# Two 48-row A loads of block 0, moved from one DMA issuing queue to two

## The chip, the cores and the metric

The kernel runs on one core of one Trainium2 chip. The metric is device time in microseconds (us) of one execution; lower is better. Before the change three runs gave a median of 473.93 us, between 473.69 and 474.05.

## The reference, cut to what matters

The input `x` is 8 batches of 256 tokens with 1024 features. Every batch b picks a low-rank adapter (rank 16) by `itok_B_3_7[b]`; the adapted activations go through a gated feed-forward network whose inputs are rounded to 8 bits; the result is added to `x`.

```python
def cond(x, A, B, ids):                    # A: 8 x 1024 x 16, B: 8 x 16 x 1024
    Bx = jnp.einsum('bni,bri->bnr', x, B[ids])
    return jnp.einsum('bnr,bor->bno', Bx, A[ids])

def linear(x, w_q, in_scale, w_scale):     # fp8 rounding of the input
    x_q = jnp.clip(x / in_scale, -448, 448).astype(jnp.float8_e4m3fn)
    return jnp.einsum('bsh,ih->bsi', x_q.astype(jnp.float32) * in_scale, w_q * w_scale)

h = cond(x, A, B, ids)
hidden = jax.nn.silu(linear(h, gate_w, ...)) * linear(h, up_w, ...)   # 2752 wide
return x + linear(hidden, down_w, ...)
```

## The kernel before

The 2048 tokens are four blocks of 512 (t = 0 to 3), two batches to a block. Features stand on the 128 partitions, so a block of `x` is eight slices (k = 0 to 7) of 128 x 512 floats. Everything is computed in transposed form. For one block the work is:

1. `bx`: B times x, summed over k = 0 to 7 (rank 16, so small matmuls). For block 0 this is `two_times_b`. It needs all of x of block 0 and the two B tiles of its two batches.
2. `bm`: VectorE and ScalarE copy `bx` out of PSUM, in two steps, to lie under the A rows (lines 570 and 574).
3. `c`: A times bm, in `two_times_a`: 32 matmuls, 64 in the trace since each float32 product is two passes. Weights are rows of `a_two[0]`. Those rows hold A of the two batches: batch 0 in rows 0 to 47, batch 1 in rows 80 to 127. Each is one load of 48 rows of 2 KB, 96 KB. The row groups are taken in the order 0, 2, 1, 3, so the first matmul needs the load of batch 0, the next one that of batch 1.
4. `xg`: ScalarE and VectorE round `c` to fp8 (lines 608 and 606).
5. `gate_up(c, t)`: for each of 22 column chunks c of the 2752, 16 matmuls of 128x128 by 512 against streamed weights `w_gu` (1 MB a chunk), then silu and a product into `hid`.
6. A last part multiplies `hid` by the down weights and adds `x`.

TensorE is busy from the start. Before the data of block 0 are there it runs fillers on ones (`pass_time` into `warm`): 14 at the start, two between k = 6 and k = 7, and six after `bx`, ahead of `c`. Matmuls keep the program's order on TensorE. On the other engines a planner at compile time chooses the order, by the program's order and by when it thinks that an instruction's inputs are there.

At the start the loads are issued by two queues. ScalarE's queue issues the adapter numbers `ids_i`, a small read `touched` of the first weights, and B of batch 0 (behind a register load of its adapter number). SyncE's queue issues all else, in the order: x slices 0-1, x slices 2-4, B of batch 1 (behind its register load), x slices 5-6, x slice 7, A of batch 1, then a second register load and A of batch 0, then the weight loads, of which the first four are halves of chunks 0 and 1. The two A loads are `load_a_two` (L398 to L402) and its two calls at L443 and L444. x slices 0-1, 2-4, 5-6 and 7 are separate loads of 512, 768, 512 and 256 KB. Ahead of the A loads GpSimd sets `a_two[0]` to zero (L384).

Each load announces its landing on a completion counter. Loads issued by ScalarE and SyncE take the counters in turn, and an issue waits, on its own queue, until the earlier load on the same counter has landed.

Of the kernel before, what the change touches and what calls it, by code (L numbers as in the profile page):

```python
# [301 lines left out]
def adaln_ffn(  # L302
# [15 lines left out]
    nc = tc.nc  # L318
# [45 lines left out]
    with ExitStack() as fast:  # L364
# [5 lines left out]
        xs = [acts.tile([P, NH, TB], F32, name=f"x{t}") for t in range(NTB)]  # L370
# [8 lines left out]
        b_two = [lora.tile([P, 2 * BROW + R], F32, name=f"b{t}") for t in range(2)]  # L379
        a_two = [lora.tile([P, H // 2], F32, name=f"a{t}") for t in range(2)]  # L380
# [7 lines left out]
        def adapter_of(batch, queue):  # L388
            return queue.value_load(ids_i[0:1, batch : batch + 1], min_val=0, max_val=7)  # L389

        def load_b(b, i, adapter, queue):
            load = queue.dma_start(  # L392
                out=b[:, i * BROW : (i + 1) * BROW], in_=b8[bass.ds(adapter * P, P), :]
            )
            if queue is nc.gpsimd:
                tc.keep_in_program_order(load)

        def load_a_two(j, adapter):  # L398
            row = 2 * 32 * j + R * j
            nc.sync.dma_start(  # L400
                out=a_two[0][row : row + 3 * R], in_=a8[bass.ds(adapter * 3 * R, 3 * R), :]
            )  # L402

# [7 lines left out]
        def load_x(t, k):  # L411
            piece, first = x_of(x4, t, k)
            ks = slice(first, first + piece.shape[1])
            nc.sync.dma_start(out=xs[t][:, ks, :], in_=piece)  # L414
# [16 lines left out]

        load_x(0, 0)
        load_x(0, 2)
        load_b(b_two[0], 0, adapter_of(0, nc.scalar), nc.scalar)
        touched = const.tile([R, R], F32, name="touched")
        nc.scalar.dma_start(
            out=touched, in_=gate_up_of(w_gu, 0).rearrange("(r g) n -> r g n", r=R)[:, 0, :R]
# [1 line left out]
        second = adapter_of(1, nc.sync)  # L439
        load_b(b_two[0], 1, second, nc.sync)  # L440
        load_x(0, 5)
        load_x(0, 7)
        load_a_two(1, second)  # L443
        load_a_two(0, adapter_of(0, nc.sync))  # L444
        for c in range(NFIRST):
            load_gate_up(c, parts=(0, 2, 4) if c < 2 else (0, 4))
        adapters = [adapter_of(2 + q, nc.gpsimd if q < 2 else nc.sync) for q in range(6)]
# [442 lines left out]
        for k in range(NH - 1):  # L890
# [23 lines left out]
            first = k % 2 == 0  # L914
# [133 lines left out]
```

## Time and profile before

| what | value |
|---|---|
| median of three runs | 473.93 us |
| the profiled execution | 473.77 us |
| its span on the core | 472.1 us |
| TensorE (PE) busy | 467.3 us, 99% of the span, 2477 matmuls |
| ScalarE (ACT) busy | 194.9 us, 41% |
| VectorE (DVE) busy | 106.5 us, 23% |
| GpSimd (POOL) busy | 16.0 us, 3% |
| bytes moved by DMA | 56.01 MB, mean 119 GB/s |
| DMA in the first 40 us | mean 371 GB/s |

The profiled execution is 1.67 us longer than its span: this much lies around what the profile covers. Times inside the profile count from the start of the span. In a line of the timeline the first number is the start, the second the duration, "x2" the instructions merged into the line, and the bracket the idle time of the engine before it and what ended that.

The loads of the start, from the timeline (issue) and the view of DMA issues (time from issue to landing):

| load | queue | issue at | issue to landing |
|---|---|---|---|
| adapter numbers | ScalarE | 0.86 | not listed; the register loads that wait for it start at 2.06 |
| x slices 0-1, 512 KB | SyncE | 0.86 | 3.4 |
| x slices 2-4, 768 KB | SyncE | 1.29 | 4.9 |
| `touched`, 1 KB | ScalarE | 1.46 | 3.8 |
| B of batch 0, 68 KB | ScalarE | 3.01 | 3.5 |
| B of batch 1, 68 KB | SyncE | 3.06 | 3.7 |
| x slices 5-6, 512 KB | SyncE | 3.46 | 4.4 |
| x slice 7, 256 KB | SyncE | 3.94 | 5.0 |
| A of batch 1, 96 KB | SyncE | 4.65 | not listed |
| A of batch 0, 96 KB | SyncE | 5.80 | 4.0 |
| chunk 0, first half, 512 KB | SyncE | 6.23 | 4.9 |

### The profile page before, as it was taken

To read this page: it belongs to the slowest core of one execution; us is meant where nothing else is said; L and a number is where in the kernel's file an instruction comes from. 1 tells how busy PE (TensorE), PEld (TensorE's weight loads), DVE (VectorE), ACT (ScalarE), POOL (GpSimd) and SP (SyncE) were. 2 spreads that over 40 slices of the span, in tenths; PEclk is the share of its full clock that TensorE was granted. 3 is DMA by queue.
4 is the path that set the end of the run, shared out by engine and by line. 5 is a ranking of instruction groups with operands and counts; after the bars stand their busy time and mean duration, and the time that the engine had idled before them with its cause. 6 is when DMAs were issued, how large, how long until landed. Compare 5 with 4: busy or idle time off the path is not lost.

```text
span 472.1 us, 5981 instructions
## 1 busy us (share of the span) xinstructions
PE 467.3 (99%) x2477; PEld 214.5 (45%) x2477; DVE 106.5 (23%) x170; ACT 194.9 (41%) x257; POOL 16.0 (3%) x32
## 2 busy tenths in 40 slices
PE   8999999999999999999999999999999999999997
PEld 4454444444444444444444444444444444444444
DVE  1314341222121212212122121231120111031031
ACT  2315258996655554553345545359112012021000
POOL 0230500000000000000000000000000000000000
PEclk9999999999999999999999999999999999999999
DMA  8999205352222211222220021132435345163031
GB/s 303 422 369 367 53 3 169 104 173 89 90 89 90 89 30 61 89 90 89 90 87 20 27 62 57 61 105 102 136 115 161 77 174 162 40 207 104 5 115 68
DMA packets 14661, 56.01 MB, mean 119 GB/s; under 512 B 1762, under 2 KB 2786, under 8 KB 11938
## 3 DMA queue, kind: packets, MB, share of 16 engines
q1 hardware_dynamic: 14256, 55.08, 34.2%
q8 instruction: 21, 0.34, 0.3%
q0 software_dynamic: 192, 0.40, 0.3%
q14 instruction: 14, 0.11, 0.1%
q10 hardware_dynamic: 178, 0.07, 0.1%
HBM read 47.15 MB, written 8.39 MB: 118 GB/s over the span
## 4 chain that ended last, share of the span: by engine, by line
PE 97%; DMA 1%; SPq 0%; issue 0%; DVE 0%
PE y L521 63%; PE yd L521 32%; PE c L521 1%; PE bx L521 1%; DMA x<-x 1%; DMA ids_i<-ids 0%; SPq L389 0%; PE warm L521 0%; SPq L392 0%; SPq L414 0%; DVE o L855 0%; PE count L521 0%
## 5 line engine op out<-in xcount | busy, mean ns | idle before, releaser
L521 PE MATMUL y<-xg,w_gu 128*128 128x512 fp8e4 x1376 | 298.6, 379 | 0.0
L521 PEld LDWEIGHTS <-w_gu 128*128 128x128 bf16 x1376 | 133.7, 98 | 162.0 <-DVE xg L606 1.6
L521 PE MATMUL yd<-hid,w_d 128*128 128x512 fp8e4 (+2 forms) x693 | 146.0, 373 | 0.0
L695 ACT ACTIVATE g<-y,gate_s 128x512 f32<-128x512 f32 (+1 forms) x88 | 59.5, 681 | 134.1 <-PE y L521 134.1
L724 DVE SCALAR_TENSOR_TENSOR hid<-y,up_by_down,g 128x512 fp8e4<-128x512 f32 x84 | 63.0, 750 | 215.9 <-PE y L521 145.7
L521 PEld LDWEIGHTS <-w_d 128*128 128x128 bf16 x693 | 66.6, 98 | 79.0 <-issue 1.7
L507 ACT ACTIVATE junk<-w_d 128x1408 bf16<-128x1408 uint16 (+1 forms) x16 | 21.2, 1323 | 88.3 <-DMA w_d<-w_d 88.2
L855 DVE SCALAR_TENSOR_TENSOR o<-yd,down_s,x 128x512 f32<-128x512 f32 x28 | 20.0, 748 | 107.5 <-PE yd L521 93.4
L507 ACT ACTIVATE junk<-w_gu 128x2048 bf16<-128x2048 uint16 (+1 forms) x22 | 41.0, 1864 | 0.0
L514 ACT ACTIVATE junk<-hid 128x2048 bf16<-128x2048 fp8e4 x21 | 40.1, 1908 | 0.6
L514 ACT ACTIVATE junk<-xg 128x2048 bf16<-128x2048 fp8e4 x8 | 15.3, 1911 | 0.3
L606 DVE TENSOR_SCALAR xg<-c,inv 128x512 fp8e4<-128x512 f32 (+1 forms) x20 | 11.7, 638 | 6.4 <-PE c L521 6.4
L608 ACT ACTIVATE xg<-c,inv 128x512 fp8e4<-128x512 f32 (+1 forms) x20 | 10.6, 601 | 4.6 <-PE c L521 4.6
L521 PE MATMUL warm<-const-bfloat16-1.0 128*128 128x512 bf16 (+1 forms) x22 | 5.9, 426 | 0.9 <-PEq L1037 0.9
L855 DVE SCALAR_TENSOR_TENSOR o<-yd,down_s,xg 128x512 f32<-128x512 f32 (+2 forms) x5 | 3.2, 644 | 12.3 <-PE yd L521 9.9
L507 ACT ACTIVATION_READ_ACCUMULATOR junk<-w_gu 128x1 f32 x22 | 4.2, 193 | 0.0
L521 PEld LDWEIGHTS <-const-bfloat16-1.0 128*128 128x128 bf16 x23 | 2.3, 118 | 4.3 <-issue 3.8
L521 PE MATMUL yd<-hid_tail,w_dt 64*128 64x512 bf16 (+1 forms) x32 | 4.2, 377 | 0.0
L724 DVE SCALAR_TENSOR_TENSOR tail<-y,up_by_down,g 64x512 fp8e4<-64x512 f32 x4 | 3.0, 756 | 4.9 <-ACT g L695 4.8
L514 ACT ACTIVATION_READ_ACCUMULATOR junk<-hid 128x1 f32 x21 | 3.9, 187 | 0.0
L521 PE MATMUL bx<-x,b_four_twice 128*32 128x256 f32 x64 | 3.7, 380 | 0.0
L521 PE MATMUL bx<-x,b 128*32 128x128 f32 x64 | 2.3, 277 | 0.9 <-DMA b<-b 0.7
(69 smaller groups left out, 56.1 us busy)
## 6 DMA issues: line engine op xcount, KB each, us to landing
w_gu<-w_gu SPq DMA_DIRECT2D x18, 1024.0 KB, 4.9
outT<-o SPq DMA_DIRECT2D x31, 256.0 KB, 2.1
w_d<-w_d SPq DMA_DIRECT2D x8, 704.0 KB, 5.1
w_gu<-w_gu SPq DMA_DIRECT2D x10, 512.0 KB, 4.9
w_d<-w_d SPq DMA_DIRECT2D x8, 640.0 KB, 3.8
x<-x SPq DMA_DIRECT2D x2, 2048.0 KB, 19.3
x<-x SPq DMA_DIRECT2D x1, 1792.0 KB, 13.8
x<-x SPq DMA_DIRECT2D x2, 512.0 KB, 3.9
```

The costliest lines, as they stand in the source:

```text
L507: nc.scalar.activation(junk_like(w), low(w), AF.Copy, accum_out=lows[:rows, column : column + 1])
L514: nc.scalar.activation(junk_like(q), q, AF.Square, accum_out=squares[:rows, column : column + 1])
L521: tc.keep_in_program_order(nc.tensor.matmul(*args, **kwargs))
L606: nc.vector.tensor_scalar(to, c, scale, None, ALU.mult, saturate=False)
L608: nc.scalar.activation(to, c, AF.Copy, scale=scale, saturate=False)
L695: nc.scalar.activation(g[rows], gates, AF.Silu, scale=gate_s[: gates.shape[0]])
L724: nc.vector.scalar_tensor_tensor(to, in0=ups, scalar=up_by_down[rows], in1=g[rows], op0=ALU.mult, op1=ALU.mult, saturate=False,)
L855: nc.vector.scalar_tensor_tensor(o, in0=y, scalar=down_s, in1=x, op0=ALU.mult, op1=ALU.add)
```

## The change

`load_a_two` takes the issuing queue as an argument. A of batch 1 stays on SyncE's queue behind all of x. A of batch 0 goes to ScalarE's queue, and uses the register that ScalarE loaded for B of batch 0, so SyncE's second register load disappears. Ahead of it ScalarE copies one element of x slice 2 into the first element of `a_two[0]`, which the load overwrites: the copy waits for x slices 2-4, and the load waits for the copy.

```diff
-        def load_a_two(j, adapter):
+        def load_a_two(j, adapter, queue):
             row = 2 * 32 * j + R * j
-            nc.sync.dma_start(
+            queue.dma_start(
                 out=a_two[0][row : row + 3 * R], in_=a8[bass.ds(adapter * 3 * R, 3 * R), :]
             )
...
-        load_b(b_two[0], 0, adapter_of(0, nc.scalar), nc.scalar)
+        first = adapter_of(0, nc.scalar)
+        load_b(b_two[0], 0, first, nc.scalar)
...
-        load_a_two(1, second)
-        load_a_two(0, adapter_of(0, nc.sync))
+        load_a_two(1, second, nc.sync)
+        nc.scalar.copy(a_two[0][:1, :1], xs[0][:1, 2, :1])
+        load_a_two(0, first, nc.scalar)
```

## The prediction

> **What bounds the kernel now.** I read the chain that ended last, first as shares on the page and then in order of time, since a change in the first 10 us matters only if the chain passes there.
>
> ```profile
> PE 97%; DMA 1%; SPq 0%; issue 0%; DVE 0%
> ```
> ```profile
> 3.94 4.99 DMA x<-x
> 8.94 0.04 issue
> 8.98 0.42 PE bx L521 x8
> 9.41 0.45 PE warm L521 x6
> 9.86 0.10 issue
> 9.96 2.19 PE c L521 x61
> 12.15 21.69 PE y L521 x100
> ```
>
> The columns are start, duration and what. The chain waits for x slice 7 (landed at 8.94), then runs on TensorE to the end of the kernel. So whatever shifts the start of `c` (9.96) shifts the end by the same amount: behind it TensorE has no idle stretch that could swallow it. The fillers take TensorE only to 9.86; the 0.10 us behind them is the one gap. The timeline and the DMA issues show what it waits for.
>
> ```profile
> 9.44 0.28 DVE L570 COPY bm<-bx 64x128 f32<-64x128 f32 x1 [2.12 <-PE bx L521]
> 9.50 0.26 ACT L570 COPY bm<-bx 64x128 f32<-64x128 f32 x1 [6.79 <-PE bx L521]
> 9.93 0.65 PEld L521 LDWEIGHTS c<-bm,a 32*128 32x128 f32 x15 [0.25 <-issue]
> ```
> ```profile
> a<-a SPq DMA_DIRECT2D x1, 96.0 KB, 4.0
> ```
>
> VectorE's copy of `bm` ends at 9.44 + 0.28 = 9.72, ScalarE's at 9.76. A of batch 0 was issued at 5.80 and took 4.0, so it landed at 9.8; the first weight load of `c` starts at 9.93, the first matmul at 9.96. A is thus the later input, if by less than 0.1 us. From landing to first matmul are 9.96 - 9.8 = 0.16 us.
>
> Third, SyncE's queue.
>
> ```profile
> 4.65 1.49 SPq L400 DMA_DIRECT2D a<-a  x2
> 6.23 0.84 SPq L424 DMA_DIRECT2D w_gu<-w_gu  x2
> ```
> ```profile
> SPq L424 <- DMA x<-x: 0.4, 1, 0.4
> ```
>
> Nothing makes a weight load depend on x but its completion counter. Counting the loads in order of issue, chunk 0's first half is the eleventh and slices 2-4 of x the third; these landed at 1.29 + 4.9 = 6.2, and the issue came at 6.23. So a load waits for the one eight before it.
>
> **The change part by part.** Terms are shifts of the start of `c`, that is of the end.
>
> Removed from SyncE: a register load and one A issue. A of batch 1's issue (median of the two 0.34) ends at about 5.0, the second A issue at 4.65 + 1.49 = 6.14, so 1.1 us of queue time come free. They gain nothing: the weight issue waits for the counter until 6.2 anyway. Should the planner let it take an earlier counter and go at 5.0, it still gains nothing: chunk 0's first half landed at 6.23 + 4.9 = 11.1 and is first used at 12.1, a cover of 1.0 us. Without that cover an earlier issue would be worth at most 1.1 us. Term: 0.
>
> x slice 7 is issued ahead of both A loads and was never behind them. The new A load could delay it only if its bytes went first: 96 KB at the 383 GB/s of the window from 7 to 8 us is 0.25 us. The bounds are 0 and +0.25, and I take 0, since the A load is issued 2.6 us after slice 7.
>
> Added on ScalarE: one copy and one DMA issue. ScalarE does no other work between its B issue (3.01, 0.39 long) and the `bm` copy at 9.50, so the instructions themselves are hidden by 2.5 us. Behind them on ScalarE wait the `bm` copies, which `c` needs; they would be late only if the issue ended after 9.50. Their start would then be the next thing late, one for one.
>
> What counts is when A of batch 0 lands. The copy waits for slices 2-4 (6.2), and starts 0.04 later, as `bx` did after slice 7: 6.26. A copy of one element is not in the trace. GpSimd's 1x1 copy takes 0.18, ScalarE's 64x128 copy 0.26; I take 0.26. The step from an engine's result to the DMA issue that waits for it is 0.03 at the end of the kernel (VectorE's last output ends at 469.53, its store is issued at 469.55) and 0.56 behind GpSimd's 1x1 copy. I take 0.03, ScalarE's other hand-overs being like it: its silu ends at 16.01, the product waiting for it starts at 16.04. The issue is then at 6.26 + 0.26 + 0.03 = 6.55, bounds 6.5 and 7.1, against 5.80 before.
>
> Issue to landing on ScalarE's queue while SyncE's is full:
>
> ```profile
> b<-b ACTq DMA_DIRECT2D x1, 68.0 KB, 3.5
> touched<-w_gu ACTq DMA_DIRECT2D x1, 1.0 KB, 3.8
> b<-b POOLq DMA_DIRECT2D x2, 68.0 KB, 6.0
> ```
>
> Even the 1 KB read took 3.8, so it is waiting, not bytes, that sets this. B of batch 0's packets moved between 5.5 and 6.0 (the DMA view of that window has 128 packets of q10, ScalarE's queue), 2.5 to 3.0 us after its issue, and it landed 0.3 us after x slices 2-4, which had been issued before it. A load on ScalarE's queue thus waits for what the other queue has already handed over. The nearest row is B's: about the same size, same queue, x ahead of it. So A lands at 6.55 + 3.5 = 10.05, and `c` starts at 10.05 + 0.16 = 10.21: **+0.25 us**. Bounds: below, A lands before the `bm` copies are done; then `c` starts at 9.72 + 0.16 = 9.88, the fillers letting go at 9.86, a gain of **0.08**. Above, 7.1 + 6.0 (GpSimd's row, its loads behind a queue of whole weight chunks) = 13.1, +3.3 us.
>
> A of batch 1 keeps its place, two instructions later in need. It moves at most earlier.
>
> The Trainium skill, page "DMA: Bandwidth & Descriptors", section "Issuing engines are not separate DMA queues", speaks against the change: loads of all issuers run on the same 16 engines and another issuer saves only sequencer time, which here is the 1.1 us that lies behind a counter. By this alone the sum would be 0. The same page, section "Queues, rings and completion order", says that an engine goes round-robin between its queues packet by packet; by that A would pass x in its turn and the sum would be the gain of 0.08, which the 3.5 and 3.8 us rows do not bear out.
>
> **Sum:** 473.77 + 0.25 = 474.02 for the profiled execution; it lies 0.16 below the median of the runs, so 474.2 in terms of medians.
>
> **Rivals.** In terms of medians:
>
> - *A lands in time.* If ScalarE's queue gets its turn during slice 7, A lands before 9.7 and the gap goes: 473.93 - 0.08 = 473.85. For it: only 96 KB, three rows for each of 16 DMA engines. Against it: both ScalarE rows of 3.5 and more.
> - *The counter wait (slower).* The new load takes its place in the counter order where the planner puts it; it waits for a copy, so it may come behind weight issues. Up to two weight issues ahead of it cost nothing, since the counters eight loads back are slices 2-4 (6.2) or earlier; behind four the counter is B of batch 1 (6.8), still harmless. Behind five it is x slices 5-6 (7.9), behind six x slice 7: issue at 8.98, landing at 8.98 + 3.5 = 12.5, `c` at 12.64, +2.7 us: 476.6; behind seven it is A of batch 1, free at about 9.35, +3.05: 477.0. It makes the kernel measurably slower from an issue after 7.25 (10.75 + 0.16 = 10.91, +0.95). For it: nothing holds the planner to the program's order between the queues, as ScalarE's `touched`, issued at 1.46 ahead of B, shows. Against it: SyncE issues a weight chunk at 15.74, which waited for TensorE, ahead of x loads that wait for nothing, so the planner thinks of SyncE as slow and busy, and would place few weight issues in the time of slices 2-4.
> - *Behind the weights.* The first weight packets are queued by 6.6, just as A is issued. Were A to land in 5.0, between the 4.0 and 6.0 rows, it would be there at 11.55, `c` at 11.7, +1.75: 475.7. For it: the DMA rate falls from 344 GB/s (8.2 to 8.7) to 205 (8.7 to 9.2), just where A would move. Against it: A of batch 0 on SyncE landed through the same stretch in 4.0.
> - *Faster by more than 0.95.* To 472.9 or less. It would need x slice 7 itself about 1 us earlier. Nothing ahead of it is touched, so only a reordered start could do it.
>
> **How the numbers follow.** 0.2% is 0.95 us, about what a measurement of this kernel can tell from no change. Forecast (+0.25, from 0 to +0.9): 0.41. In time: 0.21. Counter wait: 0.20. Behind the weights: 0.13. Faster: 0.05. Both first cases are within 0.2%: same 0.62, slower 0.33, faster 0.05. The predicted time is the forecast's, 474.2. The likeliest case's own range is 473.8 to 474.9. For 8 in 10 the range goes from 473.6 (the gain of 0.08, and runs that spread by 0.2) to 476.6, where it holds the rival behind the weights and the counter wait up to slice 7; left out are the rest of that rival, about 0.1, and the faster case.
>
> **What would show it.** A ScalarE copy at about 6.26 and its DMA issue at 6.55 confirm the waits; an issue after 7.9 is the counter rival. A landing of A near 10.05 and `c` at 10.2 confirm the size; a `c` at 9.88 is the in-time rival. x slice 7 should still land at 8.94, the first weight issue still come at 6.2 or earlier, and from `c` on all should run as before with one shift. I am wrong if that shift doesn't reach the end, or if slice 7 moves.

## The result and the profile after

The changed kernel takes 477.43 us (median of six runs, 476.0 to 477.79) against 473.93, so it is slower: the medians lie 3.5 us apart, and the ratio over all runs is 1.0066 with a 95% interval of 1.0056 to 1.0076. The forecast was 474.2, the range ended at 476.6.

The profiled execution took 477.33 us, 3.56 more than the one of before. First the chain that ended last, in order of time, in the changed kernel (start, duration, what; lines shifted by two, so L523 is the L521 of before):

```profile
1.30 4.97 DMA x<-x
6.27 0.02 issue
...
6.36 0.20 ACT a L445
6.56 0.02 issue
6.58 5.12 DMA a<-a
11.70 0.14 issue
11.84 2.78 PE c L523 x61
14.62 22.72 PE y L523 x100
...
67.08 256.09 PE y L523 x1186
```

The chain no longer runs through x slice 7. It goes from x slices 2-4 (6.27) over the one-element copy into the moved A load, which takes 5.12 us, and `c` starts behind its landing. Against the chain of before: `c` starts at 11.84 instead of 9.96 (+1.88); it takes 2.78 instead of 2.19 (+0.59); the next hundred matmuls take 22.72 instead of 21.69 (+1.03). The sum is 3.50. From there on the two traces run alike: the long stretch of `y` started at 63.57 before, now at 67.08 (+3.51), and lasts 256.09 against 256.08.

Two of the three terms are not waits: TensorE does the same work more slowly. The view by windows shows why (busy time of PE, PEld, DVE, ACT, POOL, each with its instructions, then the granted clock, the DMA share and GB/s):

```profile
10.00:11.00 1.00, 0.02 (x1) 0.00 (x0) 0.47 (x2) 0.45 (x2) 0.00 (x0) 1.00 1.07 340
11.00:12.00 1.00, 0.16 (x4) 0.19 (x5) 0.00 (x0) 0.00 (x0) 0.00 (x0) 1.00 0.99 377
12.00:13.00 1.00, 1.00 (x37) 1.00 (x40) 0.00 (x0) 0.00 (x0) 0.00 (x0) 1.00 1.02 410
13.00:14.00 1.00, 1.00 (x34) 1.00 (x30) 0.87 (x3) 1.00 (x3) 0.00 (x0) 0.63 1.03 414
14.00:15.00 1.00, 1.00 (x13) 0.50 (x9) 1.00 (x3) 1.00 (x3) 0.00 (x0) 0.50 1.13 463
15.00:16.00 1.00, 1.00 (x4) 0.41 (x3) 0.99 (x2) 0.59 (x2) 0.00 (x0) 0.50 1.03 418
16.00:17.00 1.00, 1.00 (x5) 0.36 (x3) 0.00 (x0) 0.00 (x0) 0.00 (x0) 0.66 0.94 377
```

TensorE is all but idle from 10 to 11.84, and the granted clock falls at about 13.3, after TensorE has begun again. The clock lost in these windows is 0.37 + 0.50 + 0.50 + 0.34 = 1.71, that is half speed for 3.4 us. Of the six runs four were granted 0.996 of the clock over the whole and took 477.33 to 477.79, two were granted 1.0 and took 476.0 and 476.2: 1.5 us apart. So there are two losses, a late A (+1.9) and a slow stretch of TensorE (+1.6) that four of the six runs add to it. The page's row of the granted clock, in fortieths of the span, shows the second one in a single digit:

```profile
PEclk9899999999999999999999999999999999999999
```

Why A is late is seen in the DMA packets by queue, of the changed kernel from 8 to 9.5 us (first line), from 8.6 to 9.4 (second) and from 9.5 to 10.8 (the other two). q1 is SyncE's queue, q10 ScalarE's:

```profile
q1 hardware_dynamic: 166, 0.50, 109.7%
```
```profile
q1 hardware_dynamic: 60, 0.25, 95.8%
```
```profile
q1 hardware_dynamic: 93, 0.32, 77.9%
q10 hardware_dynamic: 63, 0.10, 20.7%
```

The columns are packets, MB and share. A's 96 KB (0.10 MB on q10) do not move before 9.5, three microseconds after their issue; from 8 to 9.5 SyncE's queue moves 0.50 MB. From 8.6 to 9.4 those are packets of 4 KB throughout (0.25 MB in 60), which are weights, about half of the first weight half. From 9.5 on A's packets move among those of the weights. The first weight half was issued at 6.29 and landed 4.9 later, at 11.2; A was issued at 6.58 and landed at 11.70. In the kernel before, the window from 9.5 to 10 held weights alone (48 packets, 0.20 MB). What remained to be settled: is A late because weights were handed over ahead of it, or because ScalarE's queue is slow; and is the clock's fall a consequence of TensorE's idling?

### The profile page after: what moved, and what is told of

It is laid out like the page before. It is cut to its first block, busy times and chain, and to the rows that moved or that the text cites. A ratio compares the mean times of both kernels' runs of the same rounds, so it can differ in the third digit from the quotient of the medians.

```text
span 475.7 us, 5980 instructions
## 1 busy us (share of the span) xinstructions
PE 469.6 (99%) x2477; PEld 215.3 (45%) x2477; DVE 106.5 (22%) x170; ACT 195.1 (41%) x258; POOL 16.0 (3%) x32
## 4 chain that ended last, share of the span: by engine, by line
PE 97%; DMA 2%; SPq 0%; issue 0%; DVE 0%; ACT 0%; ACTq 0%
PE y L523 63%; PE yd L523 31%; PE c L523 1%; PE bx L523 1%; DMA a<-a 1%; DMA x<-x 1%; SPq L414 0%; DVE o L857 0%; ACT a L445 0%; ACTq L445 0%; PE count L523 0%
## 5 line engine op out<-in xcount | busy, mean ns | idle before, releaser
L523 PE MATMUL y<-xg,w_gu 128*128 128x512 fp8e4 x1376 | 299.6, 380 | 0.0
L523 PEld LDWEIGHTS <-w_gu 128*128 128x128 bf16 x1376 | 134.0, 98 | 162.9 <-issue 2.2
L523 PE MATMUL yd<-hid,w_d 128*128 128x512 fp8e4 (+2 forms) x693 | 146.0, 373 | 0.0
L523 PEld LDWEIGHTS <-w_d 128*128 128x128 bf16 x693 | 66.6, 98 | 79.0 <-issue 1.7
L523 PE MATMUL warm<-const-bfloat16-1.0 128*128 128x512 bf16 (+1 forms) x22 | 6.7, 469 | 0.9 <-PEq L1039 0.9
L523 PEld LDWEIGHTS <-const-bfloat16-1.0 128*128 128x128 bf16 x23 | 2.5, 124 | 4.7 <-issue 4.6
L523 PE MATMUL c<-bm,a 32*128 32x128 f32 x64 | 2.8, 322 | 1.8 <-DMA a<-a 1.8
L523 PE MATMUL yd<-hid_tail,w_dt 64*128 64x512 bf16 (+1 forms) x32 | 4.2, 377 | 0.0
L523 PE MATMUL bx<-x,b_four_twice 128*32 128x256 f32 x64 | 3.7, 380 | 0.0
```

The source lines that it names most:

```text
L523: tc.keep_in_program_order(nc.tensor.matmul(*args, **kwargs))
```

## The experiments

Theory W: A waits behind what is handed over before it, on whichever queue. Theory Q: it is ScalarE's queue. Theory C: idling costs the clock.

**Without the copy** (e1). ScalarE issues A as early as it can.

```diff
-        nc.scalar.copy(a_two[0][:1, :1], xs[0][:1, 2, :1])
         load_a_two(0, first, nc.scalar)
```

> The changed kernel without the one-element copy, so that ScalarE issues A of batch 0 right behind B of batch 0, at about 3.45 instead of 6.58. Theory W (the load is late because the first weight halves are already handed over when it is issued): it lands ahead of x slice 7, before 9.2; c starts between 9.86 and 10.15, slice 7 being up to 0.25 later; 473.85 to 474.2 us, clock 1.0. Theory Q (a load on ScalarE's queue takes about 5 us whatever lies ahead): landing at 3.45 + 5.1 = 8.6, the same time. If both fall, and the late c does not come from the landing of A, the time stays near 477.

Measured: 474.45 us against 473.88 on the same chip, ratio 1.0012 (1.0003 to 1.0021), clock 1.0. A was issued at 3.58 and landed 4.5 later, at 8.1. `c` no longer waits for it, but its bytes went among those of x slices 5-6 and ahead of slice 7. The chain, the timeline of TensorE (`c`), the issue view of slices 5-6 and the packets of the window from 6.2 to 7 us in e1:

```profile
3.94 5.42 DMA x<-x
9.35 0.04 issue
9.40 0.43 PE bx L522 x8
```
```profile
10.24 2.19 PE L522 MATMUL c<-bm,a 32*128 32x128 f32 x64
```
```profile
x<-x SPq DMA_DIRECT2D x1, 512.0 KB, 5.0
```
```profile
q1 hardware_dynamic: 53, 0.22, 74.6%
q10 hardware_dynamic: 47, 0.09, 32.2%
```

Slice 7 landed at 9.35 instead of 8.94, 0.41 later, and `c` started 0.28 later than before, just above what was expected. So without the copy 0.6 of the 3.5 us are left. The trace accounts for half of them, by slice 7: the span is 472.4 us against 472.1. The other half lies outside the span and stays open. Keeping A's bytes out of the way of slice 7 is what the copy is good for.

A here passed a bulk load that was issued before it: slices 5-6 went out at 3.44 and landed at 8.4, A went out 0.14 us later and landed at 8.1, packets of both moving side by side.

**Copy from x slice 0** (e4). A between the two: it is issued when slices 0-1 have landed.

```diff
-        nc.scalar.copy(a_two[0][:1, :1], xs[0][:1, 2, :1])
+        nc.scalar.copy(a_two[0][:1, :1], xs[0][:1, 0, :1])
```

> The changed kernel with the copy taking its element from x slice 0 instead of slice 2, so that it waits for slices 0-1 (4.2): A is issued by ScalarE at about 4.6, ahead of every weight issue. Theory W: it moves among x slices 5 to 7 and lands before 9.5; slice 7 is up to 0.4 later, as in e1; c starts at 9.9 to 10.35; 473.9 to 474.5 us. Theory Q: landing 4.6 + 5.1 = 9.7, the same time.

Measured: 474.3 us against 473.86, ratio 1.001 (1.0001 to 1.002). Issue at 4.47, landing 4.8 later at 9.3; slice 7 at 9.25, `c` at 10.13. As e1: ahead of the weights A costs slice 7 some 0.3 us, behind them it costs 3.5.

**The copy alone** (e2). Both loads on SyncE as before; only the copy is added, which holds A of batch 0 and everything behind it in SyncE's queue.

```diff
+        nc.scalar.copy(a_two[0][:1, :1], xs[0][:1, 2, :1])
         load_a_two(0, adapter_of(0, nc.sync))
```

> The kernel before with the one-element copy alone: both A loads on SyncE, that of batch 0 held until x slices 2-4 have landed, so issued at about 6.58, and all weight issues behind it. Theory W: ahead of every weight packet it lands 3 to 3.5 us after its issue, 9.6 to 10.1; c starts at 9.9 to 10.25; 473.9 to 474.3 us. If the issue time alone made it late (5.1 us from an issue at 6.58, whatever the queue), c starts at 11.84 and the time is 476 to 477.8. Theory Q gives the first of the two as well: together with e5 it is told apart.

Measured: 474.44 us against 473.88, ratio 1.001 (1.0001 to 1.0019). A was issued at 6.47, as late as in the changed kernel, but ahead of the first weight issue (6.85), and took 3.2 instead of 5.1. `c` was not late at all, and another wait came in its place; the median is a little above what was expected. The timeline of TensorE in e2:

```profile
9.78 2.19 PE L522 MATMUL c<-bm,a 32*128 32x128 f32 x64
12.18 1.04 PE L522 MATMUL y<-xg,w_gu 128*128 128x512 fp8e4 x4 [0.21 <-DMA w_gu<-w_gu]
```

The weights, issued 0.6 later, landed just too late for `y`, by 0.2 us. The issue time alone thus does not make A late, nor do weights that follow it within 0.4 us on its queue; what is left is what is issued before it.

**First weight half held back** (e5, then e5b). A one-element copy from x slice 5 into the weight tile makes the weight load wait until 7.9, while A's issue stays.

```diff
             cuts = [n * i // 4 for i in parts]
+            if c == 0:
+                nc.scalar.copy(w[:1, 0, :1], xs[0][:1, 5, :1])
```

> The changed kernel with the first weight half held back by a second one-element copy, from x slice 5 into the weight tile: its issue comes at about 8.2 instead of 6.29, while A of batch 0 is still issued by ScalarE at 6.58. Theory W: no weight packet is ahead of A any more; it moves right behind slice 7 and A of batch 1 and lands at 9.3 to 9.7. Theory Q: it lands at 11.7 as in the changed kernel. The time says little, since the weights themselves come later: first half landing at 12 to 13, y from about 12.5, 474 to 476 us.

Measured: 477.12 us (one run, clock 0.996). The experiment missed its aim: the planner put the second half of the chunk, which was not held, first, at 6.16. With that one half ahead A, issued at 6.45, took 4.9 and landed at 11.3. So 512 KB ahead of it are enough. TensorE idled for 1.56 us ahead of `c` here, and the clock fell again. The timeline of TensorE in e5:

```profile
11.45 3.48 PE L525 MATMUL c<-bm,a 32*128 32x128 f32 x64 [1.56 <-DMA a<-a]
```

The next kernel holds both halves.

```diff
+            if c == 0:
+                for i in (0, NH):
+                    nc.scalar.copy(w[:1, i, :1], xs[0][:1, 5, :1])
```

> As e5, but with both halves of the first weight chunk held back until x slices 5-6 have landed (in e5 the second half was free and was issued first, at 6.16). A of batch 0 is still issued by ScalarE at about 6.5; the first weight issue comes at about 8.2. Theory W: nothing but x and A of batch 1 is ahead of it; it lands at 9.3 to 9.8, some 2 us earlier than in the changed kernel. Theory Q: 11.3 to 11.8. The time is 474 to 476 us, set by the later weights.

Measured: 474.39 us (one run, clock 1.0). The issue view, the packets of the window from 8 to 9 us and TensorE's timeline of e5b:

```profile
a<-a ACTq DMA_DIRECT2D x1, 96.0 KB, 2.9
```
```profile
q10 hardware_dynamic: 64, 0.10, 34.1%
```
```profile
9.86 2.19 PE L526 MATMUL c<-bm,a 32*128 32x128 f32 x64
12.24 5.10 PE L526 MATMUL y<-xg,w_gu 128*128 128x512 fp8e4 x22 [0.19 <-DMA w_gu<-w_gu]
```

Same queue, same issue time (6.59), but A's packets move between 8 and 9 us instead of behind 9.5, and it lands at 9.5. ScalarE's queue is not slow. Theory Q falls. The engines also had less to move in that window than in the changed kernel (184 GB/s against 340), so e5b alone does not tell order from load; e2 does, on SyncE's queue.

**On SyncE behind the first half** (e6), the counterpart: nothing on ScalarE, but weights ahead.

```diff
-        load_a_two(0, adapter_of(0, nc.sync))
         for c in range(NFIRST):
-            load_gate_up(c, parts=(0, 2, 4) if c < 2 else (0, 4))
+            load_gate_up(
+                c,
+                parts=(0, 2, 4) if c < 2 else (0, 4),
+                between=(lambda: load_a_two(0, adapter_of(0, nc.sync)),) if c == 0 else (),
+            )
```

> The kernel before with A of batch 0 left on SyncE, but issued behind the first half of the first weight chunk (that half at about 5.05, A at about 6.2); ScalarE issues nothing of it. Theory W: 512 KB of weights are ahead of it, some 1.3 us at 400 GB/s more than before; it lands at 10.7 to 11.5, c starts at 10.9 to 11.7, and the time is 474.8 to 475.6, up to 477 if the clock falls. Theory Q (it is ScalarE's queue that is slow): 4.0 us after the issue as before, 10.2, c at 10.4, 474.3.

Measured: 477.68 us, ratio 1.0083 (1.0065 to 1.0101), clock 0.996 in all four runs. The issue view, the chain and TensorE's timeline of e6:

```profile
a<-a SPq DMA_DIRECT2D x1, 96.0 KB, 5.9
```
```profile
6.28 5.91 DMA a<-a
12.19 0.14 issue
12.32 3.75 PE c L524 x64
```
```profile
12.32 3.75 PE L524 MATMUL c<-bm,a 32*128 32x128 f32 x64 [2.34 <-DMA a<-a]
```

On its old queue A is even later than in the changed kernel (12.19), beyond the upper end of what was expected, and so is the time. With a weight half issued first A is late on either queue (the changed kernel, e5, e6), without one it is in time on either (e2, e5b): in this sense theory W holds from both sides. Between two queues it is not a strict order. In e1 A passed slices 5-6, issued 0.14 us before it; in the changed kernel, 0.29 us behind the weight half, it did not. What decides between the two was not tested.

**Fillers over the wait** (e3 and e7). The changed kernel, with more fillers ahead of `c`.

```diff
-        pass_time(warm, 6)
+        pass_time(warm, 36)      # e7: 20
```

> The changed kernel with 36 fillers instead of 6 ahead of c, 30 more at 0.058 us, which cover the 1.8 us that TensorE waits for A. Theory C (about 1.6 us of the loss is the granted clock, halved for 3.4 us after TensorE idled): the clock stays 1.0, c starts at about 11.9 as in the changed kernel, c and y run at full speed, and the time is 475.8 to 476.1, in every round. If the clock falls for another reason than the idle time (the late c itself, the phase of the execution), the time stays at 477.4 in most rounds.

Measured: 475.94 us (475.77 to 476.28), ratio 1.0042 (1.0028 to 1.0056), clock 0.999 to 1.0 in all five runs. The chain of e3:

```profile
6.42 5.36 DMA a<-a
11.78 0.14 issue
11.91 2.19 PE c L523 x61
```

A is as late as ever, `c` starts as late, but takes 2.19 again. More useless work on TensorE makes the changed kernel 1.5 us faster: theory C holds, and the two losses are apart. TensorE's idle time ahead of `c` was 0.3 us here.

> The changed kernel with 20 fillers instead of 6 (36 in e3): TensorE idles about 1.0 us ahead of c instead of 1.8. Theory C says that the granted clock falls after idling: if 1.0 us is short enough, the clock is 1.0 in all rounds and the time 475.8 to 476.1 as in e3; if it is not, the time is 477.4 in most rounds. No number of before tells which; a fall in some rounds would put the limit near 1 us.

Measured: 475.79 us (475.56 to 476.19), ratio 1.0034 (1.0017 to 1.0051), clock 0.999 to 1.0 in all five. The timeline of TensorE in e7:

```profile
11.72 2.19 PE L523 MATMUL c<-bm,a 32*128 32x128 f32 x64 [1.10 <-DMA a<-a]
```

An idle time of 1.1 us cost no clock in these runs.

No version beat the kernel before. The most that an earlier A can give is seen in e5b, `c` at 9.86 instead of 9.96: 0.1 us, less than the runs of before differ among themselves (0.36). The 9.78 of e2 has slice 7's products at 8.86 instead of 8.98, which is 0.12 of its 0.18. Both gave the gain back in later weights: `y` started at 12.18 and 12.24 against 12.15 before.

## Why the prediction was wrong, point by point

*What bounds the kernel; the gap of 0.10 us at 9.86 waits for A.* Right. With A there at 9.5, e5b started `c` at 9.86; 9.88 had been worked out.

*SyncE's freed 1.1 us gain nothing.* Right: the first weight issue came at 6.29, still held by x slices 2-4.

*x slice 7 keeps its time.* Right within the stated bounds: its products started at 9.14 in the changed kernel against 8.98, and at 8.94 and 8.92 in e3 and e7, which load alike, so the 0.16 us are not put down to the change. The bound of 0.25 for A's bytes ahead of it was somewhat low: e1 shows 0.41, e4 0.31.

*Copy and issue on ScalarE at 6.55.* Right: 6.58, with some luck. The copy started 0.10 late, at 6.36 instead of 6.26, and took 0.19 instead of 0.26.

*Issue to landing 3.5 us.* This is the step that failed. The row came from B of batch 0, ahead of which only x had been issued; at 6.55 the first weight half had been issued too, 0.3 us earlier. The prediction saw that, as the rival "behind the weights", and gave it 0.13. It argued against it that A on SyncE had crossed the same stretch in 4.0, but there A stood ahead of the weights. The runs give 4.9 to 5.4 with weights ahead on ScalarE's queue (the changed kernel, e3, e5, e7), 5.9 on SyncE's (e6), and 2.9 to 3.2 for the same issue time without them (e5b, e2). The rival's own 5.0 and 475.7 us are close to what e3 and e7 measured with a full clock, 475.94 and 475.79. That the nearest row fits only with the same work ahead shows at the other end too: with more of x still ahead, A took 4.5 (e1) and 4.8 (e4).

*A shift of `c` reaches the end one for one.* This is the second step that failed. It is true of the wait (+1.88), but the sum had no term for what an idle TensorE does to its clock: +0.59 in `c` and +1.03 in `y`. Every rival with a late A lacked it as well, and it puts the median 0.8 us above the range. The trace of before has no idle stretch of that length, and so no row for it.

*The counter wait.* It did not happen as described. A was issued at 6.58, right behind its copy, and waited for no counter. It turned round instead: a weight load waited for A's landing. Counted in order of issue this is chunk 3, the sixteenth, which puts A eighth, ahead of slice 7. SyncE's waits of the changed kernel:

```profile
SPq L424 <- DMA a<-a: 3.2, 1, 3.2
```

This wait is no part of the loss: the list of TensorE's waits has none for weights.

Of the Trainium skill, "Issuing engines are not separate DMA queues" on the page "DMA: Bandwidth & Descriptors" is borne out by e5b and e6 taken together: 2.9 us on ScalarE's queue, 5.9 on SyncE's, by what was ahead. The round-robin of "Queues, rings and completion order" is seen once A's packets move, 63 of them among 93 of SyncE's queue between 9.5 and 10.8, but it did not carry A past the half chunk that had been issued 0.29 us before it: 11.70 against 11.2.

## What to carry to other kernels

A small load that sits just ahead of a flood of big ones in one queue has a good place, and a second queue does not keep it: here its issue moved 0.3 us behind the first big one, and it landed 1.9 us later. So when a load is moved, compare its new issue time with that of every bulk load on any queue, and take its time to landing from a row with the same work ahead. And price a wait on TensorE's path twice, once for the wait and once for the clock behind it; fillers can save the second part.

## What the runs showed of the hardware that was not expected

An idle time of 1.8 us went with a granted clock halved for 3.4 us in the changed kernel (four of six runs by their mean clock), 2.3 us in e6 (four of four) and 1.6 us in e5 (its one run); 1.1 us in e7 and 0.3 us in e3 did so in none of five each, nor did 1.3 us ahead of `bx` in e5b (one run). The idle times are those of the one profiled execution of each kernel. The Trainium skill, page "TensorE: Matmul & The Clock Gate", Part 1, puts the fall after an idle window of about 3.4 us. The half rate and the 3.4 us at it agree with the trace; the idle time that was needed does not, it was about half of that. The page also says that the window runs freely, which would let the same idle time matter in some runs and not in others; that this is the reason for four of six was not tested. The traces fit it in one point: the fall has no fixed distance from the start of the idle time. It comes 3.2 us behind it in the changed kernel (13.26 against 10.02), 2.2 in e5 (12.12 against 9.89) and 2.4 in e6 (12.36 against 9.98), worked out from the mean clock of the window in which it falls: 0.63 from 13 to 14, 0.56 and 0.68 from 12 to 13.
